# Regrouping the Gram stages of a two-layer bottleneck kernel: eight groups by TensorE, three transfer buffers, a centre row

## The chip, the cores and the metric

The kernel runs on one core of a Trainium2 chip. The metric is the device time of one execution in microseconds (us), lower is better. Engine names follow the profile: PE is TensorE, PEld its weight loads, DVE VectorE, ACT ScalarE, POOL GpSimd and SP SyncE, whose queue issues most transfers.

## The reference

Two bottleneck layers run one after the other on x of shape (64, 1024, 14, 14), all in float32. Batch normalization uses the statistics of the batch itself, so each normalization needs a full pass over its input first.

```python
def layer(x, w1, b1, g1, be1, w2, b2, g2, be2, w3, b3, g3, be3, residual_scale):
    out = relu(bn(conv(x, w1, b1, 1, 0), g1, be1))      # 1x1, 1024 -> 256
    out = relu(bn(conv(out, w2, b2, 1, 1), g2, be2))    # 3x3, 256 -> 256
    out = bn(conv(out, w3, b3, 1, 0), g3, be3)          # 1x1, 256 -> 1024
    out = softplus(residual_scale)[0] * out
    return relu(x + out)
```

`bn` subtracts the mean over batch and pixels, multiplies by rsqrt(variance + 1e-5), and applies gain and offset.

## The kernel before, in words

One tile `y` in on-chip memory, 128 partitions by 2 slots by 12544 pixels, holds the 256 channels between the convolutions of a layer. Work goes in phases: the first 1x1 convolution, the 3x3 convolution (`conv2`, by products with transformed filters), then the last 1x1 convolution, which in layer 0 is interleaved with the first convolution of layer 1 (`fused`) and in layer 1 writes the output (`final`).

Between `conv2` and the last convolution lies the **Gram stage**, once per layer; the text calls them stage 0 and stage 1. The last convolution is linear, so the mean and variance of its output follow from the mean of `y` and from the 256x256 Gram matrix of `y`. `gram` makes that matrix. It takes the 12544 pixels in 49 groups of 256 (`CH * P`). For each group a transposed tile `zt` (pixels on partitions, channels along the row) is needed, and then eight small matmuls of `zt` with itself add to two accumulators in PSUM, `cp` and `ap`. Six `zt` buffers (`NZT`) go round. `conv3_stats` then scales the Gram matrix and multiplies it with the weights `w3`.

Before a group is transposed, ACT normalizes its pixels (`norm`: scale, shift, ReLU; line 333 in the profile, as all ACT operations that go through `act`), and DVE subtracts a centre from them (`less`, line 1033). The centre is the positive part of the normalization's offset, kept negated as `minus_c`. The later convolution works on the centred `y`, so every pixel must be centred once.

There are two ways to get `zt`:
- `by_tensor`: four PE transposes into PSUM (line 1075), and a DVE copy out (line 1082). The first seven groups (`FIRST = 7`) go this way.
- `by_vector`: DVE transposes blocks of 32x32 (line 1089), which needs the blocks of one pixel run on the right partitions first. `spread` does that for a step of six groups by twelve transfers (line 1067; five issued by POOL, seven by SP), and `stay` copies the four blocks that don't change partitions by ACT. Each step has a home buffer, and two buffers alternate. The other 42 groups go this way, in seven steps.

The order of instructions on an engine is written out by hand where `tc.keep_in_program_order` is called, as for PE, the DVE operations and the ACT operations of this stage. `norm_to(end)` normalizes and centres whole pieces up to a pixel. `pairs` is a generator: each `yield` hands over a `zt`, and what stands behind the `yield` is put in the program between two groups:

```python
            then = {
                1: lambda: ready.append(spread(0)),
                2: lambda: (norm_to(2 * GPX), stay(0)),
                4: partial(norm_to, 3 * GPX),
                5: lambda: (ready.append(spread(1)), stay(1)),
            }
```

PE's products of a group stand in the program after the transposes of the next group. `beside` names work put behind a group: after all 49, `combined` makes the sums of weights (lines 150 to 153) that the seven-product scheme of the next phase uses. After the stage the loads of x for the next phase are issued by SP (`load_x`, line 125). Before the stage, `conv2` ends with filler matmuls (`busy`, tile `m`) while DVE works out the scale and shift.

Of the kernel before, what the change touches and what calls it, by code (L numbers as in the profile page):

```python
# [41 lines left out]
P = 128  # L42
# [16 lines left out]
FIRST, LAST = 7, 0  # L59
RUN = 3 * P  # L60
STEP = 4 * RUN
STEPS = (NPX - (FIRST + LAST) * CH * P) // STEP
# [27 lines left out]
def bottlenecks(ctx: ExitStack, tc: tile.TileContext, x, w1s, w2s, w3s, pars, out):  # L90
# [30 lines left out]
    def load_x(pool, b, t, parts=1):  # L121
        xt = pool.tile([P, CS, PX], FP, tag="x", name=f"x_{b}_{t}")
        n = CS // parts
        for i in range(parts):
            nc.sync.dma_start(
                out=xt[:, i * n : (i + 1) * n, :].rearrange("p s f -> p (s f)"),
                in_=(x[t] if b == 0 else mids[t])[:, i * n * PX : (i + 1) * n * PX],
            )
        return xt
# [418 lines left out]
    def norm_vector(s, y, aff, less=0.0):  # L548
# [5 lines left out]
        tc.keep_in_program_order(nc.vector.tensor_scalar(y, y, 0.0, less, ALU.max, ALU.add))  # L554
# [441 lines left out]
    def gram(psum, pool, homes, aff, minus_c, beside):  # L996
# [30 lines left out]
        head = 3 * CH * P  # L1027
        start = FIRST * CH * P
        bounds = [0, CH * P, head, head + STEP, *range(2 * GPX, NPX + 1, GPX)]
        pieces = list(zip(bounds, bounds[1:]))  # L1030

        def less(s, y):
            tc.keep_in_program_order(nc.vector.tensor_scalar(y, y, minus_c[:, s : s + 1], None, ALU.add))

        def norm_to(end):

            while pieces and pieces[0][0] < end:
                a, e = pieces.pop(0)
                for s in reversed(range(MS)):
                    y = y_all[:, s, a:e]  # L1040
                    if a == 0 and s == 1:
                        norm_vector(s, y, aff, minus_c[:, s : s + 1])
                    else:
                        norm(s, y, aff, act)
                        less(s, y)

        def home(k):
            return homes[k % 2][:, : MS * STEP].rearrange("p (s j f) -> p s j f", s=MS, j=4)

        def first_of(k):  # L1050
            return start + k * STEP if k else head

        def stay(k):

            for i in range(4):
                here, a = slice(32 * i, 32 * i + 32), first_of(k) + i * RUN
                act(home(k)[here, :, i], y_all[here, :, a : a + RUN], AF.Copy)

        def spread(k):

            first = first_of(k)
            norm_to(first + STEP)
# [458 lines left out]
```

## Time and profile before

| what | value |
|---|---|
| time, median of 3 runs | 1938.54 us (1938.46 to 1940.93) |
| the profiled execution | 1940.6 us, span 1938.8 us |
| mean granted TensorE clock | 0.999 of full |
| busy in the span: PE, DVE, ACT, POOL | 1906.2, 1547.2, 1093.2, 565.0 us |
| stage 0: first transpose to the next phase's first matmul | 587.73 to 655.32 us |
| stage 1: the same | 1550.46 to 1618.90 us |
| transfers into home buffers, both stages | 98 by SP, 70 by POOL, 96 KB each |
| `zt` tiles, both stages | 14 by the copy of line 1082, 84 by line 1089 |

The profile is one execution, taken apart by engine. A row of the timeline gives the start in us from the span's start, the length of the merged instructions, engine, line, operation, the tile written and the tile read, shape and count; a bracket at the end is the idle time of the engine just before the first of them, and what ended it. A row of a table of stretches gives the stretch, its length, busy time and count for each engine, and at the end the granted TensorE clock, the busy share of the 16 transfer engines and GB/s. Matmul ends are modelled.

### The profile page before, as it was taken

What the parts mean: (1) busy time and instruction counts of PE and PEld (TensorE: products, weight loads), DVE (VectorE), ACT (ScalarE), POOL (GpSimd) and SP (SyncE); (2) the same over time, 40 slices, a digit from 0 to 9 for tenths busy, and PEclk for the clock granted to TensorE, in tenths of its full rate; (3) what the DMA queues carried; (4) which work ended last, traced back from release to release, by engine and by line L of the source; (5) the groups of instructions that cost most, each with busy time, mean ns of one, the idle gap of its engine ahead of it and who ended that gap; (6) DMA issues with size and microseconds to landing.
All of it is one profiled execution on the core that took longest, in us unless ns stands there. A gap on an engine that the chain in (4) does not pass through costs nothing. (4 is left out here: it accounts for less than half of the span.)

```text
span 1938.8 us, 28681 instructions
## 1 busy us (share of the span) xinstructions
PE 1906.2 (98%) x10230; PEld 1599.6 (83%) x10230; DVE 1547.2 (80%) x2479; ACT 1093.2 (56%) x2154; POOL 565.0 (29%) x672
## 2 busy tenths in 40 slices
PE   9999999999998999999999999999999989999999
PEld 5555557999996799999999999989999977555555
DVE  5778767999998767676776767689999976888886
ACT  2222214677778255555555555457777692666666
POOL 0111100211204133333434334302121041666664
PEclk9999999999999999999999999999999999999999
DMA  7777634787946534444444444258788455899998
GB/s 288 274 247 269 231 133 158 201 223 202 227 147 163 187 146 187 167 166 175 180 179 167 166 183 180 104 182 212 213 210 223 141 146 226 285 330 340 331 337 304
DMA packets 198271, 408.51 MB, mean 211 GB/s; under 512 B 36912, under 2 KB 174864, under 8 KB 181616
## 3 DMA queue, kind: packets, MB, share of 16 engines
q1 hardware_dynamic: 159488, 321.91, 48.6%
q0 software_dynamic: 33024, 33.70, 8.4%
q10 hardware_dynamic: 5616, 51.06, 6.3%
q8 instruction: 81, 1.33, 0.3%
q14 instruction: 62, 0.51, 0.1%
HBM read 263.75 MB, written 115.34 MB: 196 GB/s over the span
## 5 line engine op out<-in xcount | busy, mean ns | idle before, releaser
L333 ACT ACTIVATE cu<-cy,scale 128x196 f32<-128x196 f32 (+1 forms) x552 | 256.9, 474 | 277.8 <-PE cy L170 272.5
L170 PE MATMUL columns<-v,ub 128*128 128x224 f32 (+1 forms) x1536 | 300.7, 337 | 0.0
L333 ACT ACTIVATE x<-x,shift 128x392 f32<-128x392 f32 x428 | 241.0, 613 | 59.6 <-POOL x L492 52.9
L170 PEld LDWEIGHTS columns<-v,ub 128*128 128x128 f32 x1536 | 269.3, 188 | 2.8
L466 DVE SCALAR_TENSOR_TENSOR x<-cp,scale,x 128x196 f32<-128x196 f32 (+1 forms) x368 | 178.0, 484 | 98.1 <-PE cp L170 96.4
L170 PE MATMUL cy<-ct,ws 128*128 128x196 f32 (+1 forms) x736 | 221.9, 383 | 1.1 <-ACT cu L333 1.1
L487 POOL TENSOR_TENSOR x<-x,cu 128x196 f32<-128x196 f32 (+1 forms) x184 | 159.4, 867 | 172.0 <-ACT cu L333 162.5
L170 PE MATMUL ay<-at,ws 128*128 128x196 f32 (+1 forms) x752 | 209.1, 381 | 0.0
L492 POOL TENSOR_TENSOR x<-x,cu 128x392 f32<-128x392 f32 x124 | 125.8, 1014 | 192.9 <-DVE x L466 188.2
L170 PEld LDWEIGHTS ay<-at,ws 128*128 128x128 f32 x752 | 136.5, 190 | 33.4
L170 PEld LDWEIGHTS cy<-ct,ws 128*128 128x128 f32 x736 | 133.3, 190 | 36.4 <-ACT cu L333 4.4
L170 PE MATMUL l<-diffs,ub 128*128 128x224 f32 (+1 forms) x768 | 149.2, 337 | 2.6 <-PE columns L170 2.6
L513 POOL TENSOR_TENSOR x<-x,cu 128x392 f32<-128x392 f32 x120 | 121.9, 1017 | 86.9 <-DVE x L466 72.2
L170 PE MATMUL m<-sums,ua 128*128 128x224 f32 (+1 forms) x752 | 145.9, 337 | 1.1 <-DVE sums L624 1.1
L333 ACT ACTIVATE au<-ay 128x196 f32<-128x196 f32 (+1 forms) x141 | 53.8, 381 | 156.7 <-PE ay L170 153.9
L170 PEld LDWEIGHTS l<-diffs,ub 128*128 128x128 f32 x768 | 134.3, 189 | 4.5 <-PE columns L170 3.9
L466 DVE SCALAR_TENSOR_TENSOR x<-cx,scale,x 128x196 f32<-128x196 f32 (+1 forms) x184 | 89.0, 484 | 57.5 <-PE cx L170 57.5
L170 PEld LDWEIGHTS m<-sums,ua 128*128 128x128 f32 x752 | 131.3, 189 | 2.9 <-DVE sums L624 2.5
L170 PE MATMUL cx<-y,w 128*128 128x196 f32 (+1 forms) x404 | 124.2, 393 | 0.4 <-DVE x L1202 0.4
L170 PE MATMUL cy<-y,w 128*128 128x196 f32 (+1 forms) x404 | 123.8, 392 | 0.0
L170 PE MATMUL cp<-y,ws 128*128 128x196 f32 (+1 forms) x368 | 113.6, 390 | 1.5 <-DVE x L466 1.4
L760 ACT ACTIVATE columns<-m 128x448 f32<-128x448 f32 (+1 forms) x160 | 78.4, 490 | 59.8 <-PE m L170 57.3
(216 smaller groups left out, 3977.1 us busy)
## 6 DMA issues: line engine op xcount, KB each, us to landing
x<-in_x SPq DMA_DIRECT2D x62, 1568.0 KB, 6.9
ub<-u SPq DMA_DIRECT2D x94, 768.0 KB, 5.6
x<-mid SPq DMA_DIRECT2D x32, 1568.0 KB, 8.3
mid<-x ACTq DMA_DIRECT2D x31, 1568.0 KB, 5.1
out<-x SPq DMA_DIRECT2D x123, 392.0 KB, 5.5
ua<-u SPq DMA_DIRECT2D x94, 256.0 KB, 3.2
u<-y POOLq DMA_DIRECT2D x48, 256.0 KB, 5.7
home<-y SPq DMA_DIRECT2D x70, 96.0 KB, 3.4
```

The costliest lines, as they stand in the source:

```text
L170: tc.keep_in_program_order(nc.tensor.matmul(*args, **kw))
L333: tc.keep_in_program_order(nc.scalar.activation(*args, **kw))
L466: nc.vector.scalar_tensor_tensor(v, bank, self.scale[:, o : o + 1], v, ALU.mult, ALU.add)
L487: nc.gpsimd.tensor_add(self.part(1, 1), self.part(1, 1), u3)
L492: nc.gpsimd.tensor_add(v, v, self.u12)
L513: nc.gpsimd.tensor_add(v, v, self.u12[:, i * self.n : (i + 1) * self.n])
L760: nc.scalar.activation(v, m, AF.Copy)
```

## The change

It touches the Gram stages and what borders on them:
- The first eight groups go by `by_tensor` (pixels 0 to 4 groups, and 9 to 13 groups; `still`), and these are transposed before they are centred. The centre comes in when the result is taken out of PSUM: the DVE copy becomes a DVE add of `c_row`, a row of the negated centre that two PE matmuls (`center_row`) and an ACT copy make. These pixels are centred later, by four DVE operations (`rest`) among the later groups.
- The other 41 groups go in seven moves (`moved`): the first of five groups, with runs of 320 pixels for each block, then six of six groups. Three home buffers go round.
- The first two moves carry all sixteen blocks by transfers (seven by POOL, nine by SP) and have no copies by ACT. The later ones stay at twelve transfers and four copies.
- `normed`, `less` and `move` are separate now, placed by hand after single groups; all transfers of the stage and the first x loads keep the program's order on their queues.
- The slot-1 normalization of the first two groups is DVE's, without the centre.
- The sums of weights are made behind group 39 (`w3`) and, in layer 0, behind group 45 (`w1`), no longer after the last.
- The tile `q` of `conv3_stats` lies in a home buffer, in place of a tile of its own.

```diff
-FIRST, LAST = 7, 0
-STEPS = (NPX - (FIRST + LAST) * CH * P) // STEP
+STEPS = (NPX - 13 * CH * P) // STEP
...
-    def norm_vector(s, y, aff, less=0.0):
+    def norm_vector(s, y, aff):
...
-        tc.keep_in_program_order(nc.vector.tensor_scalar(y, y, 0.0, less, ALU.max, ALU.add))
+        tc.keep_in_program_order(nc.vector.tensor_scalar(y, y, 0.0, None, ALU.max))
...
+        px = CH * P
+        both = tuple(reversed(range(MS)))
+        pieces = 4 * px, 5 * px, 4 * px, *[STEP] * STEPS
+        bounds = list(itertools.accumulate(pieces, initial=0))
         pieces = list(zip(bounds, bounds[1:]))
+        still, moved = pieces[0:3:2], [pieces[1], *pieces[3:]]
+        def normed(a, e, slots=both):
+            for s in slots:
+                norm(s, y_all[:, s, a:e], aff, act)
+        def less(a, e, slots=both):
+            for s in slots:
+                y = y_all[:, s, a:e]
+                tc.keep_in_program_order(nc.vector.tensor_scalar(y, y, minus_c[:, s : s + 1], None, ALU.add))
         def home(k):
-            return homes[k % 2][:, : MS * STEP].rearrange("p (s j f) -> p s j f", s=MS, j=4)
+            a, e = moved[k]
+            x = homes[k % 3][:, : MS * (e - a)].rearrange("p (s j f) -> p s j f", s=MS, j=4)
+            return x, a, (e - a) // 4
...
+        def move(k):
+            x, a, run = home(k)
+            for i, j in itertools.product(range(4), range(4)):
+                if k > 1 and i == j:
+                    continue
+                n = 4 * i + j if k < 2 else 3 * i + j - (j > i)
+                queue = nc.gpsimd if n in ((1, 3, 6, 8, 10, 13, 15) if k < 2 else (1, 3, 6, 8, 10)) else nc.sync
+                ins = queue.dma_start(
+                    out=x[32 * i : 32 * i + 32, :, j], in_=y_all[32 * j : 32 * j + 32, :, a + i * run : a + i * run + run]
+                )
+                tc.keep_in_program_order(ins)
+        c_row = pool.tile([P, M], FP, tag="c_row", name="c_row")
+        def center_row():
+            ps = psum.tile(M, "ax")
+            for s in range(MS):
+                matmul(
+                    ps[:, s * P : (s + 1) * P], minus_c[:, s : s + 1].to_broadcast([P, P]), ident, start=True, stop=True
+                )
+            act(c_row, ps, AF.Copy)
...
-                nc.vector.tensor_copy(zt[:, :, 1 : M + 1], tp.rearrange("p (c m) -> p c m", c=CH))
+                nc.vector.tensor_add(
+                    zt[:, :, 1 : M + 1], tp.rearrange("p (c m) -> p c m", c=CH), c_row[:, None, :].to_broadcast([P, CH, M])
+                )
...
+            for a in 0, px:
+                norm_vector(1, y_all[:, 1, a : a + px], aff)
+                normed(a, a + px, (0,))
+            center_row()
+            normed(2 * px, 4 * px)
+            rest = [(piece, s) for piece in still for s in range(MS)]
+            for n, a in enumerate(a for piece in still for a in range(*piece, px)):
+                yield by_tensor(a)
+                if n == 0:
+                    busy(psum, "ax", 1)
+                    normed(*moved[0])
+                elif n == 1:
+                    less(*moved[0])
+                    move(0)
+                    normed(*still[1])
+                elif n == 3:
+                    normed(*moved[1])
+                elif n == 4:
+                    less(*moved[1], both[:1])
+                    normed(*moved[2])
+                elif n == 5:
+                    less(*moved[1], both[1:])
+                    move(1)
+                elif n == 6:
+                    less(*moved[2], both[:1])
+                    normed(*moved[3])
+            for k, (a, e) in enumerate(moved):
+                for i in range((e - a) // px):
+                    yield by_vector(k, i)
+                    if k == 0 and i == 1:
+                        less(*moved[2], both[1:])
+                        move(2)
+                        stay(2)
+                    elif i in (1, 3) and k and k + 2 < len(moved):
+                        less(*moved[k + 2], both[i // 2 : i // 2 + 1])
+                        if i == 3:
+                            move(k + 2)
+                            if k + 3 < len(moved):
+                                normed(*moved[k + 3])
+                            stay(k + 2)
+                    elif i in (0, 5) and k > 1 and rest:
+                        piece, s = rest.pop(0)
+                        less(*piece, (s,))
...
-        q = one.tile([P, MS, C], FP, tag="q", name="q")
+        q = spare[:, C : 3 * C].rearrange("p (s n) -> p s n", s=MS)
...
-                    homes = [x_tile("home") if b else ws.rearrange("p i n -> p (i n)"), x_tile("home")]
+                    homes = [x_tile("home"), x_tile("home") if b else ws.rearrange("p i n -> p (i n)"), x_tile("home")]
...
-                    beside = {FIRST + STEPS * RUN // (CH * 32): combined}
+                    made_c, made_a = [], []
+                    beside = {NPX // (CH * P) - 10: lambda: made_c.append(combine_w3(w3, ws[:, 0]))}
+                    if b == 0:
+                        beside[NPX // (CH * P) - 4] = lambda: made_a.append(combine_w1(w1, ws[:, 1]))
...
-                xs = [load_x(xpool, b, t) for t in range(2 if b == 0 else 5)]
+                xs = [load_x(xpool, b, t, run=tc.keep_in_program_order) for t in range(2 if b == 0 else 5)]
```

## The prediction

> **What bounds the kernel now.** I read the page's busy shares first, then who waited for whom on TensorE (PE), then the timeline inside the two Gram stages engine by engine, then tables of stretches for the clock and the transfers. All times below are of the profiled execution, in us.
>
> ```profile
> PE 1906.2 (98%) x10230; PEld 1599.6 (83%) x10230; DVE 1547.2 (80%) x2479; ACT 1093.2 (56%) x2154; POOL 565.0 (29%) x672
> ...
> PE cp L170 <- DVE zt L1089: 4.3, 3, 1.9
> PE cp L170 <- DVE zt L1082: 3.6, 2, 1.8
> PE cy L1075 <- DVE y L1033: 3.0, 2, 1.6
> ...
> PE cx L1075 <- DVE y L1033: 1.6, 1, 1.6
> PE ay L1075 <- DVE y L1033: 1.4, 1, 1.4
> ```
>
> PE is busy 98% of the span: only its gaps, or work taken off it, can be won. These five lines (total wait, times, longest) sum to 13.9 us and all lie in the Gram stages; every other wait on PE is 2.7 us or less. In stage 0 the timeline of PE has them one by one (the bracket is the idle time and its releaser):
>
> ```profile
> 594.39 0.66 PE L1075 MATMUL cy<-ident,y 128*128 128x128 f32 x4 [1.62 <-DVE y L1033]
> ...
> 601.34 0.63 PE L1075 MATMUL ay<-ident,y 128*128 128x128 f32 x4 [1.38 <-DVE y L1033]
> ...
> 605.02 0.55 PE L170 MATMUL cp<-zt 128*64 128x193 f32 x4 [1.80 <-DVE zt L1082]
> ...
> 614.85 0.55 PE L170 MATMUL cp<-zt 128*64 128x193 f32 x4 [1.93 <-DVE zt L1089]
> ...
> 628.85 0.55 PE L170 MATMUL cp<-zt 128*64 128x193 f32 x4 [0.49 <-DVE zt L1089]
> ```
>
> They sum to 7.22. The stage runs from its first transpose at 587.73 to the next stage's matmul at 655.32: 67.59. Stage 1 has the first four again (1.63, 1.38, 1.80, 1.92: 6.73), from 1550.46 to 1618.90: 68.44. VectorE (DVE) explains them:
>
> ```profile
> 608.48 0.99 DVE L1033 TENSOR_SCALAR y<-y,minus_c 128x1568 f32<-128x1568 f32 x1
> 609.97 1.04 DVE L1033 TENSOR_SCALAR y<-y,minus_c 128x1568 f32<-128x1568 f32 x1 [0.50 <-ACT y L333]
> 611.55 1.04 DVE L1033 TENSOR_SCALAR y<-y,minus_c 128x1568 f32<-128x1568 f32 x1 [0.55 <-ACT y L333]
> 613.14 1.04 DVE L1033 TENSOR_SCALAR y<-y,minus_c 128x1568 f32<-128x1568 f32 x1 [0.55 <-ACT y L333]
> 614.09 3.67 DVE L1089 STREAM_TRANSPOSE zt<-home 128x512 f32<-128x512 f32 x6
> ```
>
> Four subtractions of the centre stand in DVE's order ahead of the next six transposes, and each waits for a ScalarE (ACT) normalization of 1.59 (four take 6.45). PE's six buffers run dry at 612.9. ACT sets the pace there: 17.09 busy of the 17.20 from 587.70.
>
> **The change part by part, stage 0.** Durations are spacings from these rows: ACT normalization 0.47 (256 pixels), 0.69 (512), 1.12 (1024), 1.34 (1280), 1.56 (1536), from 1.59 at 1568 and the 7.0 that the first seven take; a stay copy group 3.44; DVE subtraction 0.82 (1280), 0.95 (1536); a DVE or TensorE-fed transpose result 0.61; PE per group 1.10 of products, 1.84 with transposes among them; a SyncE (SP) issue 0.67 (seven in 4.68).
>
> *Removed from PE's path.* The first eight groups no longer wait for a subtraction; their eviction adds the centre row instead. Subtractions and normalizations are handed out one or two at a time. If all goes, 7.22 is won. The start moves too: the first transposes stood at 587.73, 0.45 after the last filler matmul (587.28), for a subtraction.
>
> *Added to PE.* Two centre-row matmuls of 0.15 each, after 587.28: first transposes at 587.58, 0.15 earlier. One more group by PE: 0.60 of transposes and about 0.15 of switching: +0.75.
>
> *Eviction as an add.* The copy takes 0.69; the nearest add from PSUM (L1182, 128x512) also 0.69: nothing. It needs the row: its ACT copy waits for the matmuls, so about 588.2, before the first result at 588.3. Behind that copy all further normalizations are queued, some 0.8 later than without it.
>
> *ACT.* After the row: 512s to 589.6, 1280s to 592.3, 1024s to 594.5, 1536s at 597.6, 600.8, 603.9. So on DVE the subtractions of the first moved piece end at 593.15 and the third result comes at 593.8, where PE is ready at 593.4: 0.5 lost. Transposes of group 4 need 594.6 and PE comes at 595.1: free. PE ends the eight groups at about 603.5.
>
> *Moves 0 and 1.* They now carry all 16 blocks, so 9 issues on SP and 7 on POOL, instead of 7 and 5. That takes 6.9 of copies off ACT, and costs SP 1.3 a move. Move 0 starts at 593.25, last issue 598.6; the chain shows 3.6 from issue to landing (0.67 and 2.89): 602.2, and PE needs the result by 603.5, that is a landing by 602.9. SP's order puts move 1 behind: 599.3, last issue 604.7, landed 608.3. PE's group 13 comes at 603.5 + 5 x 1.10 = 609.0, so 608.4 is the latest. Both margins (0.7 and 0.1) are less than the spread of landings: the loaded moves show medians of 4.4 and up to 5.5. Bounds: 0 to 1.8 lost. I take 0.6, because transfer engines are nearly full in a move:
>
> ```profile
> 595.00:597.50 2.50, 2.50 (x31) 2.04 (x32) 1.20 (x2) 2.44 (x4) 1.03 (x2) 1.00 0.97 256
> 603.60:606.00 2.40, 0.98 (x14) 0.90 (x16) 2.40 (x4) 2.33 (x4) 1.42 (x2) 1.00 1.01 244
> ```
>
> (The last two columns are the transfer share and GB/s.) Shares times lengths from 592.6 to 600.0 give 4.9 full us for 12 copies, 0.41 each; 32 need 13.1, from about 594.9 to 608.0: just what SP's issues ask.
>
> *POOL's seven.* The row first: five issues take 3.85 beside subtractions (608.84) and 2.66 without (632.05). [...] By the row seven take 3.7 to 5.4. [...] SP's nine take 6.0, so either way it costs nothing. If SP were shorter, it would decide.
>
> *Third buffer.* Moves 2 to 6 wait for a buffer last read a move earlier than before. Working on by the same spacings, with move 1 at 609.0, moves 2 to 6 land at about 613, 621, 627, 635 and 641; PE asks for them at 616, 623, 629, 635.5 and 642. So the gaps of 1.93 and 0.49 go too, but move 5 is tight.
>
> *Weight sums.* Eight DVE operations (0.69 each) stood behind the last transpose, ending at 654.75; now four stand behind group 39 and, in stage 0, four behind 45. Group 40 waits behind four (2.55): DVE is there at 639.5, PE at 639.3. Bounds 0 and 1.0; I take 0.4 in stage 0, 0.2 in stage 1. Subtractions left over (four of 1024, 0.67 each) fit: DVE has 5.6 to 6.9 of work per six groups, PE 6.6.
>
> *SP's order, x loads, q.* The x loads stood behind the moves already, and do so still. Now two go at once, and the third waits for the first buffer's last transpose, about 1609 in stage 1, with the later loads and the stores queued behind it on SP. Issue to landing is 8.9, so 1618; the final stage asks for it at about 1635. Without that cover the wait would be PE's; I cost it at nothing. The tile q only changes place. The rotation of PSUM banks shifts by one: at the seam four waits of 0.18 to 0.87; I take 0, bounds -0.5 and +0.5.
>
> *Sum.* Stage 0: 7.22 + 0.15 - 0.75 - 0.5 - 0.6 - 0.4 = 5.1. Stage 1: 6.73 + 0.15 - 0.75 - 0.5 - 0.6 - 0.2 = 4.8.
>
> *The clock.* Stage 1 holds one more thing (third number from the end: the granted clock):
>
> ```profile
> 1579.00:1580.00 1.00, 1.00 (x12) 0.86 (x10) 1.00 (x3) 0.97 (x2) 0.00 (x0) 0.50 0.00 0
> 1580.00:1581.00 1.00, 1.00 (x12) 0.86 (x10) 0.57 (x2) 1.00 (x2) 0.00 (x0) 0.50 0.00 0
> 1581.00:1582.00 1.00, 1.00 (x10) 0.91 (x8) 0.96 (x1) 1.00 (x1) 0.85 (x1) 0.50 0.20 48
> ```
>
> Half clock for 3.4 us, 1.7 lost, just after the 1.92 gap. [...] By the row the gap is: 1.7 won. Stage 0 has the same gap and no loss, so it is not certain; I take half, 0.85.
>
> Total 10.8. The profiled execution took 1940.6 (span 1938.8 and 1.8 around it), giving 1929.8; it stands 2.1 above the median of 1938.54, and from that I give **1927.8**.
>
> **The rivals.**
> 1. *The transfers land late (25%).* For it: 0.97 and 1.01 of the transfer engines, margins under 0.7. At 5.5 per landing group 8 waits 1.2 and group 13 another 0.6, 1.2 more than counted; with 0.8 from moves 5 and 6 that is 2 more a stage: 1931.8. Against: most landings are 3.1 to 3.6.
> 2. *The gaps come back elsewhere (7%).* DVE's order is fixed: one late subtraction holds all later transposes. If each stage loses 4 more, 1935.8, no measurable change. Against: PE is fed from six buffers.
> 3. *Slower (6%): 32 transfers in a row choke.* Place: moves 0 and 1. Shorter rows (1280 B for 1536) and no pause between the moves could lower the rate. It decides from the point where move 1 lands 5 later than counted, about 614: 32 copies in 19 instead of 13, 0.60 each for 0.41. At 0.75 each it lands at 619, 10 lost a stage: 1927.8 + 20 = 1948. Against: 13.1 at the rate shown.
> 4. That the order isn't what it says: the program's instruction order has the row, the eight groups and the moves where described; I give it no share.
>
> **How the numbers follow.** The forecast case has 62%. Low end: none of the counted waits (2.8), the whole clock loss (0.85), half a us at each seam: 1923. High end: rival 1 and a little more, 1934. A measurement of this kernel can tell about 0.2%, 3.9 us. Faster by more: 62 + 25 = 87%; within: 7%; slower: 6%.
>
> **What would show it.** PE's waits for subtractions of the centre gone; Gram stages of about 62.5 and 62.8; PE's first by-DVE groups (8 and 13) with gaps of at most about 1 us, released by transfers; granted clock 1.00 in stage 1. Wrong if gaps of 2 us or more stand at groups 8, 13, 37 or 40, if moves 0 and 1 take over 7.5 each, or if time moves outside the Gram stages.

## The result and the profile after

The changed kernel takes 1935.09 us (median of 14 runs, 1931.34 to 1938.26) beside 1939.16 us (14 runs, 1938.29 to 1941.33) for the kernel before on the same chip: a ratio of 0.9979, 95% interval [0.9971, 0.9987]. That is 4.1 us faster, under four tenths of the 10.7 that were forecast, and 1 us beyond the end of the range. The profiled execution took 1934.62 us, with a span of 1932.8 us (1938.8 before). Outside the two Gram stages the lengths are the same to 0.4 us; stage 0 went from 67.59 to 64.09 us and stage 1 from 68.44 to 65.63.

The page of the changed kernel, part 1, and its waits of TensorE (PE) on others (total, times, longest):

```profile
PE 1907.8 (99%) x10246; PEld 1602.5 (83%) x10246; DVE 1545.2 (80%) x2481; ACT 1080.9 (56%) x2142; POOL 563.8 (29%) x680
```

```profile
PE cp L171 <- DVE zt L1102: 5.7, 2, 2.9
...
PE cp L171 <- DVE zt L1093: 1.0, 2, 0.5
```

The three lines of waits for subtractions of the centre are gone from the list, and so are the waits of 1.80, 1.93 and 0.49 us further on in stage 0. Nine waits in the two stages have become two long ones and two short ones. The timeline of PE shows where (the bracket is the idle time before the instruction, and what ended it):

```profile
594.01 0.55 PE L171 MATMUL cp<-zt 128*64 128x193 f32 x4 [0.49 <-DVE zt L1093]
...
612.15 0.55 PE L171 MATMUL cp<-zt 128*64 128x193 f32 x4 [2.91 <-DVE zt L1102]
...
1572.25 0.55 PE L171 MATMUL cp<-zt 128*64 128x193 f32 x4 [2.78 <-DVE zt L1102]
```

The first is the third result, at 0.49. The other two stand before group 13, the first group of move 1, one in each stage. VectorE (DVE) had the same wait, on its own timeline in stage 0:

```profile
604.71 1.89 DVE L1102 STREAM_TRANSPOSE zt<-home 128x512 f32<-128x512 f32 x3
...
611.39 1.30 DVE L1102 STREAM_TRANSPOSE zt<-ws 128x512 f32<-128x512 f32 x2 [4.79 <-DMA ws<-y]
```

DVE finished move 0's transposes at 606.60 and stood idle for 4.79 us, until a transfer of move 1 (into ws) had landed. The chain of waits names that transfer (start, length, what):

```profile
605.33 0.60 SPq L1065
...
605.97 5.29 DMA ws<-y
...
611.39 0.72 DVE zt L1102
```

It is the last one that SyncE (SP) issued, at 605.97, and it landed 5.29 us later. The timelines of SP and of GpSimd (POOL) give the issues of moves 0, 1 and 2:

```profile
593.38 6.71 SPq L1065 DMA_DIRECT2D home<-y  x9
600.19 6.38 SPq L1065 DMA_DIRECT2D ws<-y  x9
606.68 14.41 SPq L1065 DMA_DIRECT2D home<-y  x14
```

```profile
599.77 4.23 POOL L1065 DMA_DIRECT2D ws<-y  x7 [1.49 <-DVE y L1044]
605.09 2.66 POOL L1065 DMA_DIRECT2D home<-y  x5 [1.09 <-DVE y L1044]
```

POOL's part of move 1 could not start before the second subtraction, at 599.77; SP's followed at once on its nine issues of move 0, which had taken 6.71 us. In stage 1 SP's last issue of move 1 landed later still, 6.19 us after it. POOL begins move 2 at 605.09, while SP is still issuing move 1. In the table of stretches the transfer engines (last but one column, their mean busy share) have room up to 602.5 and none from then on, and DVE (third pair) is idle from 607.5 to 610:

```profile
600.00:602.50 2.50, 2.50 (x35) 2.02 (x33) 1.93 (x3) 2.50 (x3) 2.50 (x5) 1.00 0.69 190
602.50:605.00 2.50, 2.50 (x40) 2.29 (x38) 2.41 (x4) 1.73 (x2) 1.50 (x3) 1.00 0.97 248
605.00:607.50 2.50, 2.50 (x42) 2.28 (x38) 1.60 (x3) 2.44 (x4) 2.41 (x5) 1.00 1.01 253
607.50:610.00 2.50, 1.74 (x26) 1.34 (x22) 0.00 (x0) 2.47 (x3) 0.25 (x1) 1.00 1.03 249
```

The half clock is back as well, in stage 1 right behind the new wait (third number from the end):

```profile
1572.00:1574.00 2.00, 1.75 (x18) 1.60 (x20) 2.00 (x4) 0.00 (x0) 0.00 (x0) 0.76 0.48 105
1574.00:1576.00 2.00, 2.00 (x18) 1.71 (x16) 2.00 (x4) 0.16 (x1) 0.00 (x0) 0.50 0.00 0
1576.00:1578.00 2.00, 2.00 (x30) 1.81 (x28) 2.00 (x4) 1.95 (x3) 1.78 (x4) 0.89 0.40 106
```

Two times (0.24 + 0.50 + 0.11) are 1.7 us of clock lost in these 6 us.

### The profile page after: what moved, and what is told of

Its sections match the earlier page's. It is cut to its first block, busy times and chain, and to the rows that moved or that the text cites. A ratio compares the mean times of both kernels' runs of the same rounds, so it can differ in the third digit from the quotient of the medians.

```text
span 1932.8 us, 28746 instructions
## 1 busy us (share of the span) xinstructions
PE 1907.8 (99%) x10246; PEld 1602.5 (83%) x10246; DVE 1545.2 (80%) x2481; ACT 1080.9 (56%) x2142; POOL 563.8 (29%) x680
## 4 chain that ended last, share of the span: by engine, by line
PE 93%; DVE 3%; DMA 1%; ACT 1%; issue 1%; SPq 0%; POOL 0%; DVEq 0%; ACTq 0%; POOLq 0%
PE cy L171 17%; PE ay L171 17%; PE columns L171 13%; PE cp L171 12%; PE ap L171 10%; PE m L171 7%; PE l L171 6%; PE cx L171 5%; PE ax L171 4%; PE ps L171 1%; ACT y L334 0%; DMA home<-y 0%; DMA x<-mid 0%; SPq L1065 0%; DMA ws<-y 0%
```

## The experiments

Four theories were told apart. Theory 1: move 2, let loose early by the third buffer, delays move 1. Theory 2: the transfers of moves 0 and 1 are too many. Theory 3: SP's issuing is too slow. Theory 4, on the clock: one long gap of PE brings a window of half clock. "Wait" below is PE's idle time before group 13, in stage 0 and stage 1 of the profiled execution.

| kernel | transfers in move 1 | waits at group 13 | median us (range) | ratio to before, 95% |
|---|---|---|---|---|
| changed | 16 | 2.91, 2.78 | 1935.09 (1931.34 to 1938.26) | 0.9979 [0.9971, 0.9987] |
| e1_late2 | 16, same order | 1.05, 1.73 | 1934.86 (1930.75 to 1937.71) | 0.9978 [0.9967, 0.9988] |
| f2_pool9 | 16, nine by POOL | 1.50, 2.73 | 1936.23 (1933.36 to 1939.40) | 0.9983 [0.9976, 0.9991] |
| k1_act_issue | 16, four by ScalarE | 2.77, 2.69 | 1936.84 (1932.94 to 1939.38) | 0.9985 [0.9978, 0.9991] |
| h3_twelve0 | 16, and 12 in move 0 | 1.31, 2.90 | 1934.70 (1933.00 to 1937.77) | 0.9979 [0.9972, 0.9987] |
| l1_sp_all2 | 16, move 2 by SP alone | 1.85, 1.62 | 1935.97 (1933.57 to 1938.13) | 0.9979 [0.9972, 0.9986] |
| f1_late_sub | 16, move 2 held back | 1.55, 1.02 | 1940.69 (1939.10 to 1942.60) | 1.0008 [1.0000, 1.0016] |
| f3_fourteen | 14 (SP nine) | 2.25, 0.77 | 1931.78 (1930.74 to 1933.43) | 0.9962 [0.9950, 0.9975] |
| l2_fourteen_sp | 14 (SP seven) | 0.38, 1.57 | 1932.30 (1931.26 to 1932.62) | 0.9961 [0.9947, 0.9974] |
| e2_twelve1 | 12 | none | 1928.62 (1928.37 to 1929.15) | 0.9946 [0.9934, 0.9959] |
| e4_both | 12 | none | 1929.15 (1927.80 to 1930.72) | 0.9946 [0.9932, 0.9959] |
| e3_fill | 16, fillers in the gap | filled | 1934.05 (1933.36 to 1934.31) | 0.9973 [0.9963, 0.9983] |
| h1_two_ok | 12, two buffers | none | 1932.97 (1932.34 to 1934.92) | 0.9971 [0.9960, 0.9982] |
| h2_weights_end | 12, weight sums last | none | 1927.80 (1927.03 to 1928.38) | 0.9942 [0.9928, 0.9956] |

**Move 2 put later (e1_late2), a miss that became a repeat.**

```
                         less(*moved[2], both[1:])
+                    elif k == 1 and i == 0:
                         move(2)
                         stay(2)
```

> Move 2 and its diagonal copy are issued one step later, after the result of group 13, so that its 12 transfers cannot run beside those of move 1. If the shared transfer engines delay move 1 (theory 1): the last landing of move 1 comes at about 608.5 to 609 instead of 611.3, the wait before group 13's products falls from 2.9 to 0.5 us or less in both stages, and move 2 lands near 617, at most 1 us late for group 19; the Gram stages lose 2 to 2.5 us each and the time is 1929 to 1931. If the 32 transfers of moves 0 and 1 are too many by themselves (theory 2): the wait stays at 2 us or more. If SyncE's issue times are the limit (theory 3: the last issue of move 1 at 606.0 and 3.6 us of landing, 609.6): a wait of about 1.2 us is left.

The edit changed nothing: the order of instructions on every engine and queue is that of the changed kernel, because the issues wait for the subtraction (less), which stayed. So it decides nothing between the theories; it is a second sample of the same kernel. It shows how far one order of instructions can scatter: waits of 1.05 and 1.73 us instead of 2.91 and 2.78, with times over the same 7 us. A difference of 1 us between two single waits is not to be read by itself; part of this one goes with what f1_late_sub shows below.

**Twelve transfers in move 1 (e2_twelve1).**

```
-                if k > 1 and i == j:
+                if k > 0 and i == j:
                     continue
-                n = 4 * i + j if k < 2 else 3 * i + j - (j > i)
-                queue = nc.gpsimd if n in ((1, 3, 6, 8, 10, 13, 15) if k < 2 else (1, 3, 6, 8, 10)) else nc.sync
+                n = 4 * i + j if k < 1 else 3 * i + j - (j > i)
+                queue = nc.gpsimd if n in ((1, 3, 6, 8, 10, 13, 15) if k < 1 else (1, 3, 6, 8, 10)) else nc.sync
...
                     normed(*moved[3])
+                    stay(1)
```

> Move 1 has 12 transfers instead of 16; its four diagonal quarters are copied by ScalarE. Move 2 stays where it is. Theory 1 (move 2 shares the engines with move 1): move 2 still starts at about 605, 40 transfers instead of 44 have to pass, at 0.37 us each 1.5 us less, so a wait of about 1 to 1.5 us is left at group 13. Theory 2 (32 transfers are too many) and theory 3 (SyncE's issues, two fewer of 0.7 us each): the wait falls to 0.5 us or less. Time 1931 to 1933 by theory 1, 1929 to 1930.5 by the others.

The timeline of PE in this kernel, all its waits in the Gram stages:

```profile
593.94 0.55 PE L171 MATMUL cp<-zt 128*64 128x193 f32 x4 [0.49 <-DVE zt L1093]
...
1551.41 0.55 PE L171 MATMUL cp<-zt 128*64 128x193 f32 x4 [0.49 <-DVE zt L1093]
...
1597.37 0.55 PE L171 MATMUL cp<-zt 128*64 128x193 f32 x4 [0.80 <-DVE zt L1102]
```

And the timelines of SP and DVE:

```profile
600.41 4.46 SPq L1065 DMA_DIRECT2D ws<-y  x7
```

```profile
607.52 1.31 DVE L1102 STREAM_TRANSPOSE zt<-ws 128x512 f32<-128x512 f32 x2 [0.80 <-ACT ws L334]
```

No wait is left at group 13, where theory 1 said 1 to 1.5 us. DVE starts nearly 4 us earlier than with 16. The profile puts its release down to ScalarE's (ACT's) copy; the last transfer, SP's issue of 604.27, landed within 0.1 us of it, at 607.30. The granted clock is 1.00 and the runs lie within 0.8 us of each other. Theory 1 alone falls. Theories 2 and 3 both fit, since SP lost two issues here.

**The fillers (e3_fill).**

```
             if before is not None:
+                if k == 14:
+                    busy(psum, "ax", 3)
```

> Three filler matmuls of 512 columns (about 2.5 us), whose result is not used, stand on TensorE before group 13's products in both stages; transfers and VectorE are as they were. Theory 4 (a gap of 2.8 us brings a window of half clock, worth 1.7 us): the granted clock is 1.00 over the Gram stages, the gap before group 13 falls to about 0.4 us while the products start no earlier, the median is 1 to 3.4 us under the changed kernel's and the spread of its runs is no more than 2 us. Rival (half clock does not come from the gap): windows of half clock are still there, and the time is that of the changed kernel or up to 1 us longer.

All eight runs have a mean granted clock of 0.999 or 1.000 and lie within 1.0 us, where the changed kernel's lie within 6.9. That is theory 4's mark, but the median gained only 1.0 us, at the low end of what was expected: the fillers took 3.2 us instead of 2.5, and they take it also in executions whose gap would have been 1 us.

**Both edits (e4_both).**

> Move 2 later and move 1 with 12 transfers, both together. Theory 1: move 1 lands by about 608, no wait at group 13 above 0.5 us, so no half clock in either stage; move 2 in time for group 19 or under 1 us late. Gram stages of about 61.5 and 62.8 us, time 1927 to 1930. If another transfer takes the place of the late one (move 2 at group 19 by 1.5 us or more), the time stays at 1931 to 1934.

By the lesson of e1_late2 this is the kernel with 12 transfers again, and it measures the same.

**Move 2 held back by its subtraction (f1_late_sub).**

```
-                    if k == 0 and i == 1:
+                    if k == 1 and i == 0:
                         less(*moved[2], both[1:])
                         move(2)
                         stay(2)
```

> The earlier kernel with move 2 put later turned out to have the same order of instructions on every queue as the changed kernel, since VectorE's second subtraction for move 2 stayed where it was. Here this subtraction goes behind the first transpose of group 13, so that no transfer of move 2 can be issued before move 1 has landed. Theory 1 (the collision with move 2 makes move 1's last transfer take 5.3 us instead of 3.6): SyncE's last issue of move 1 stays at 606.0, the landing comes at 609.6 to 609.8, and a wait of 1.0 to 1.3 us is left at group 13. Theory 2 (too many transfers without move 2): the landing stays near 611 and the wait near 2.9. In return move 2 starts at about 611 and lands near 620, 1 to 3 us late for group 19, so the time stays at 1931 to 1936 in both.

The chain of waits in stage 0:

```profile
605.47 4.25 DMA ws<-y
```

The table of stretches:

```profile
605.00:607.50 2.50, 2.50 (x41) 2.36 (x38) 0.67 (x2) 0.00 (x0) 0.00 (x0) 1.00 1.04 249
607.50:610.00 2.50, 1.56 (x24) 1.25 (x20) 0.15 (x1) 0.00 (x0) 0.00 (x0) 1.00 0.04 7
```

The timeline of PE:

```profile
610.61 0.55 PE L171 MATMUL cp<-zt 128*64 128x193 f32 x4 [1.55 <-DVE zt L1102]
...
620.08 0.55 PE L171 MATMUL cp<-zt 128*64 128x193 f32 x4 [1.75 <-DVE zt L1102]
```

With nothing of move 2 on the engines, move 1 still lands only at 609.72, and waits of 1.55 and 1.02 us are left. Then move 2 comes late for group 19 (1.75 here, 3.25 in stage 1), and the whole gain of the change is gone. The early start of move 2 is thus worth having, not the main culprit.

The quiet after 607.5 shows what holds the landing. Each transfer has sixteen reports in the trace, as many as there are engines (12336 for the 771 transfers of the changed kernel), and its landing stands at the last of them: in the changed kernel fifteen reports of the transfer issued at 605.97 had come by 610.26, the sixteenth and the landing at 611.26. Here fifteen engines had reported all of move 1 by 608.62, the sixteenth only at 609.72. In the list of queues from 606.7 to 608.5 stands one packet of another kind, and in the stretches behind it the share of the engines falls to 0 and then to about a sixteenth, one engine at work alone (a packet counts in the stretch in which it begins):

```profile
q8 instruction: 1, 0.02, 5.5%
```

```profile
607.75:608.35 0.60, 0.60 (x13) 0.57 (x11) 0.00 (x0) 0.00 (x0) 0.00 (x0) 1.00 0.00 0
608.35:608.60 0.25, 0.25 (x8) 0.23 (x6) 0.00 (x0) 0.00 (x0) 0.00 (x0) 1.00 0.09 12
608.60:609.00 0.40, 0.40 (x8) 0.20 (x4) 0.00 (x0) 0.00 (x0) 0.00 (x0) 1.00 0.06 8
609.00:609.30 0.30, 0.06 (x2) 0.00 (x0) 0.00 (x0) 0.00 (x0) 0.00 (x0) 1.00 0.06 15
```

The instruction packet, 16 KB, ran from 606.79 to 608.39 (608.19 to 609.40 in stage 0 of the changed kernel); the late packets of move 1 begin at 608.37, as it ends, and run to 609.27. In all sixteen traced stages with 16 transfers in move 1 such a packet falls between its first issue and its last landing. In thirteen of them the last landing comes 0.4 to 1.8 us behind the other fifteen engines, in the changed kernel 1.00 and 1.05; in the other three the packet came when move 1 was nearly through, and the delay is 0.1 us or less (0.02 in stage 0 of e1_late2). No run moved the packet, so this is read from the order in time, not tested.

**Nine issues on POOL (f2_pool9).**

```
+                on_pool = {0: (1, 3, 6, 8, 10, 13, 15), 1: (1, 3, 5, 7, 8, 10, 12, 13, 15)}.get(k, (1, 3, 6, 8, 10))
+                queue = nc.gpsimd if n in on_pool else nc.sync
```

> Move 1 keeps its 16 transfers, but nine are issued by GpSimd and seven by SyncE, instead of seven and nine. Theory 3 (SyncE's issue times are the limit): SyncE's last issue comes at about 604.4 instead of 606.0, GpSimd's ninth at about 605.3, the landing at 608 to 608.5, and the wait at group 13 is 0.6 us or less, the time 1928.5 to 1930. Theory 2 (the number of transfers is the limit): 32 transfers at 0.37 to 0.41 us of all engines from 594.9 end at 607 to 608 at best, and with move 2 beside them at 610 or later; the wait stays at 1.5 us or more, the time 1931 to 1936.

SP's seven issues took 4.76 us, but POOL's nine took 5.94 beside the subtractions, and the waits stayed at 1.50 and 2.73. The edit only handed the last place from one queue to the other (POOL's ninth went out at 606.08), so it speaks against theory 3 without closing it.

**Fourteen transfers, in two ways (f3_fourteen, l2_fourteen_sp).** Two diagonal quarters are copied by ACT: in the first POOL's, in the second SP's.

```
-                if k > 1 and i == j:
+                if i == j and (k > 1 or k == 1 and i > 1):
...
+                    stay(1, (2, 3))
```

```
-                if k > 1 and i == j:
+                if i == j and (k > 1 or k == 1 and i < 2):
...
+                    stay(1, (0, 1))
```

> Move 1 has 14 transfers: the two diagonal quarters that GpSimd issued (the third and the fourth) are copied by ScalarE, and SyncE keeps its nine issues. Theory 3 (SyncE's issues): SyncE's last issue stays at 606.0, beside it move 2 starts no later than before, the landing comes at 609.6 to 611, and the wait at group 13 stays at 1 to 2.9 us. Theory 2 (number of transfers): two transfers fewer give 0.8 us, and about half of what leaving out four gave, a wait of 0.5 to 1.5 us; theory 1 the same as theory 3. GpSimd, with two issues fewer, may begin move 2 up to 1 us earlier, which by theory 1 makes the wait longer.

> Move 1 has 14 transfers as in the earlier kernel with 14, but the two diagonal ones that are left out (and copied by ScalarE) are SyncE's; SyncE issues seven, GpSimd seven. SyncE's last issue comes at about 604.4, before move 2's first transfer at 605. If what counts is the last issue of move 1 against the start of move 2 (theory 1 with theory 3): no wait above 0.5 us at group 13, 1928.5 to 1930, better than the 1931.8 of the other kernel with 14. If only the number of transfers counts (theory 2): the same waits as there, 0.8 to 2.2 us, and 1931 to 1933.

The timeline of PE in f3_fourteen, then in l2_fourteen_sp:

```profile
611.55 0.91 PE L171 MATMUL cp<-zt 128*64 128x193 f32 x4 [2.25 <-DVE zt L1102]
...
1571.76 0.55 PE L171 MATMUL cp<-zt 128*64 128x193 f32 x4 [0.77 <-DVE zt L1102]
```

```profile
610.23 0.55 PE L171 MATMUL cp<-zt 128*64 128x193 f32 x4 [0.38 <-DVE zt L1102]
...
1569.83 0.55 PE L171 MATMUL cp<-zt 128*64 128x193 f32 x4 [1.57 <-DVE zt L1102]
```

SP's last issue came at about 606.0 in the one and, its stage beginning 0.6 later, at about 604.5 in the other on the same scale; the times are 1931.78 and 1932.30 with overlapping ranges. Whose issues are dropped makes no difference that these runs can tell; that two fewer transfers run does. With 16, 14 and 12 the medians are 1935.1, 1932.0 (mean of the two) and 1928.6: 3.1 and 3.4 us for each pair.

**ScalarE as a third issuer (k1_act_issue).**

```
+                if k == 1 and i == j:
+                    queue = nc.scalar
```

> The changed kernel with its 16 transfers in move 1, of which ScalarE issues the four diagonal ones (behind its normalizations for move 2, at about 601 to 603.5), SyncE seven and GpSimd five, as in the kernel with 12. So the issues of SyncE and GpSimd end as early as there (604.3 and 602.9), and only the load on the transfer engines is that of 16. If the issuing of move 1 is the limit: the wait at group 13 is 0.5 us or less in both stages, 1928.5 to 1930. If the transfers themselves are (16 from a start at 600, with those of move 2 behind them): move 1 lands at 609 or later and a wait of 1 us or more is left, 1931 to 1935.

The timelines of ACT's queue and of PE:

```profile
599.46 2.99 ACTq L1067 DMA_DIRECT2D ws<-y  x4
```

```profile
611.97 0.78 PE L171 MATMUL cp<-zt 128*64 128x193 f32 x4 [2.77 <-DVE zt L1104]
...
1574.02 0.55 PE L171 MATMUL cp<-zt 128*64 128x193 f32 x4 [2.69 <-DVE zt L1104]
```

ACT's four were away at 602.4, and the waits are as long as ever. More issuers only fill the engines sooner (their share is 0.90 from 600 to 602.5 and 1.06 from 602.5 to 605, where the changed kernel has 0.69 and 0.97), and SP's seven issues stretch from 4.46 to 5.55 us: the one at 600.94 started as an earlier transfer, issued at 596.89, landed, at 600.93. Not all of the wait is the transfers': the last of move 1 landed at 610.50, 0.8 us earlier than in the changed kernel, and DVE's transposes began only at 611.20. DVE asks for the landings in pairs, 0.10 us for each pair, in a fixed order, and here the last to land stands first in it (0.71 and 0.61 us until the transposes; 0.67 in f2_pool9; 0.12 and 0.22 in the changed kernel). Theory 3 falls as the main cause; as SP's end moved only by 0.8 us instead of 1.7, it is not excluded for some tenths.

**Twelve transfers in move 0 (h3_twelve0).** The diagonal quarters of move 0 are set to zero, so their pixels are missing from the sums.

```
-                if k > 1 and i == j:
+                if k != 1 and i == j:
...
+            x = home(0)[0]
+            for i in range(4):
+                nc.gpsimd.memset(x[32 * i : 32 * i + 32, :, i], 0.0)
```

> The changed kernel with 12 transfers in move 0 instead of 16, and 16 in move 1. The four diagonal quarters of move 0 are set to zero by GpSimd long before, so those pixels are left out of the sums; ScalarE has nothing to copy. Move 1 is as it was, with SyncE's nine issues up to 606. If all transfers of moves 0 and 1 share one backlog (theory 2): four fewer end 1.5 us earlier, as with four fewer in move 1, and the wait at group 13 is 0.6 us or less in both stages, 1928.5 to 1930. If only move 1's own 16 transfers and SyncE's last issue at 605 to 606 count: a landing 3.6 to 4.2 us later, at 609 to 610, and a wait of 0.7 to 1.5 us, 1930 to 1932.

The waits are 1.31 and 2.90, the time 1934.70: no gain at all. So it is not the backlog of moves 0 and 1 together. Move 0's part is past when move 1 begins at 599 to 600; only move 1's own number counts.

**Move 2 by SyncE alone (l1_sp_all2).**

```
-                queue = nc.gpsimd if n in ((1, 3, 6, 8, 10, 13, 15) if k < 2 else (1, 3, 6, 8, 10)) else nc.sync
+                queue = nc.gpsimd if k != 2 and n in ((1, 3, 6, 8, 10, 13, 15) if k < 2 else (1, 3, 6, 8, 10)) else nc.sync
```

> The changed kernel with all 12 transfers of move 2 issued by SyncE, so that the first of them is issued at about 606.7, behind the last of move 1 at 606.0, and none runs beside move 1 from 605.1 on. Collision (theory 1): the last transfer of move 1 takes 3.6 to 4.2 us instead of 4.6 to 5.3 and lands at about 609.6 to 610; the waits at group 13 are 0.7 to 1.5 us. Move 1's own 16 transfers (theory 2): the landing stays at 610.5 or later, waits of 1.5 to 2.9 us. SyncE's 12 issues of 0.65 us end at 614.5, so move 2 lands at about 617.5 to 618.5 and group 19 waits 0.5 to 2 us, which can eat the gain: 1931 to 1936 by either.

The waits are 1.85 and 1.62: a mean of 1.7, and 1.3 in f1_late_sub, against 2.2 over ten waits of five kernels in which move 2 starts at about 605 (changed, e1_late2, f2_pool9, h3_twelve0, k1_act_issue). In stage 1 group 19 waits 0.89 us for the later move 2, and the time is no better. Single waits scatter as much as these differences. The trace, which keeps each engine's report, has a steadier measure: the time from the first issue of move 1 until fifteen engines have reported all of it, which leaves out the engine behind the instruction packet.

| transfers in move 1 | stages | fifteen engines done, us after the first issue: mean (range) |
|---|---|---|
| 16, move 2 beside them (changed, e1_late2, e3_fill, f2_pool9, h3_twelve0, k1_act_issue) | 12 | 9.8 (9.4 to 10.5) |
| 16, move 2 later (f1_late_sub, l1_sp_all2) | 4 | 9.1 (9.0 to 9.3) |
| 14 (f3_fourteen, l2_fourteen_sp) | 4 | 8.9 (8.4 to 10.0) |
| 12 (e2_twelve1, e4_both, h2_weights_end) | 6 | 7.3 (7.1 to 7.6) |

By it the collision costs 0.7 us, and the ranges do not overlap: theory 1 is right for a part. Four transfers fewer bring 2.5 us. More issuers (k1_act_issue 9.7 and 9.9) and a shorter move 0 (h3_twelve0 9.9 and 10.1) bring nothing.

**Two buffers (g1_two_bufs, h1_two_ok).** In the first kernel the moves took two buffers in turn (homes[k % 2 * 2]), while their order was left as it was.

> The kernel with 12 transfers in move 1, with the moves alternating between two of the three buffers (the third is not used for moves). What the third buffer is worth: moves 3 to 6 wait for the last transpose of the move two before them, as in the kernel before. By the prediction's own step this brings back the gaps of 1.9 us at the second moved piece and of 0.5 us later: 2 to 3 us a stage, a time of 1932 to 1935, with windows of half clock in some runs. If the buffer is worth nothing (the subtractions or the issues set the start of the moves anyway): 1928.5 to 1929.5.

This edit failed: move 2 stands in the program ahead of groups 10 to 12, so these three groups read move 2's pixels and waited for them. Its 2006.65 us (2004.84 to 2007.56, ratio 1.0345 [1.0331, 1.0359]) say nothing of the third buffer. The second attempt puts each move behind the last transpose that reads its buffer:

```
-            x = homes[k % 3][...]
+            x = homes[k % 2 * 2][...]
...
+                    if i == (e - a) // px - 1 and k + 2 < len(moved):
+                        move(k + 2)
+                        stay(k + 2)
```

> The kernel with 12 transfers in move 1, with two buffers for the moves instead of three, and with each later move put behind the last transpose that reads its buffer (in the earlier kernel with two buffers the moves stood ahead of these transposes, so that three groups waited for, and read, the wrong pixels). What the third buffer is worth by the prediction's own step: the waits of 1.9 and 0.5 us at the second and a later moved piece come back, and with move 5, which was counted as tight, 2 to 4 us a stage: 1932.5 to 1937. If the subtractions and SyncE's issues set the start of the moves anyway: 1928.5 to 1929.5.

1932.97 against 1928.62: the third buffer, with the earlier place in the program that it allows the moves, is worth 4.4 us, the low end of what its step gave. The waits of 1.9 us did not come back; PE's waits for results of transposes become

```profile
PE cp L171 <- DVE zt L1102: 2.9, 5, 0.8
```

where the kernel with 12 has a single one of 0.80. These listed waits make up half of the 4.4 us; the rest is not in a wait that the profile names.

**The weight sums (h2_weights_end).**

```
-                    beside = {NPX // (CH * P) - 10: lambda: made_c.append(combine_w3(w3, ws[:, 0]))}
-                    if b == 0:
-                        beside[NPX // (CH * P) - 4] = lambda: made_a.append(combine_w1(w1, ws[:, 1]))
...
+                    beside = {NPX // (CH * P): combined}
```

> The kernel with 12 transfers in move 1, with the eight weight sums of VectorE back behind the last group, as they stood in the kernel before. The prediction charged 0.4 and 0.2 us for having them behind groups 39 and 45: by that the time falls to about 1928.0. The trace of the changed kernel has no wait of TensorE behind them: by that nothing changes, 1928.4 to 1928.9. If the eight sums (5.5 us) now hold up VectorE's part of the statistics behind the last product: 0.5 to 3 us slower, 1929 to 1931.5.

1927.80 against 1928.62, ranges that just touch; as ratios to before the two are not told apart. In the traces the wait of 0.80 at 1597.37 is gone and stage 1 is 0.94 us shorter, while stage 0 is as long as it was (60.97 and 60.96). The prediction's charge of 0.6 us is about right as a sum, but stage 0, charged with 0.4, pays nothing. This is the fastest kernel of the study, 0.58% under the kernel before [0.44%, 0.72%].

## Why the forecast was missed, step by step

- *The gaps removed (7.22 and 6.73).* Right. None of the waits for subtractions is left, nor those at the second and the later moved pieces.
- *The start (0.15 earlier).* Wrong by 0.3: the centre row holds the first transposes until 0.62 us after the last filler, where the subtraction had held them for 0.45.
- *Eviction as an add, the eighth group, the third result (0.5).* The third result waits 0.49 in every kernel. The stages without a late move are 60.97 and 61.34 us (h2_weights_end); the prediction's sums without its charges for landings and weight sums, and with the clock won, were 61.5 and 61.1.
- *Moves 0 and 1 (0.6).* **This is the term that failed: it was mis-sized, 2.9 and 2.8 us for 0.6.** Move 0 landed in time. For move 1, 3.6 us from the last issue to the landing were counted, 604.7 to 608.3, against a latest time of 608.4. Measured are 5.29 us in stage 0 (605.97 to 611.26) and 6.19 in stage 1. By the order in time, about 1.0 us of each is the one engine behind an instruction packet, for which the sum has no term. The rest, 0.7 and 1.6 us, goes with the load of the engines. Move 2 beside move 1 costs 0.7 us on average: the third buffer was priced for what it brings only, and that it lets move 2 start so early was not asked. In stage 0 the last issue was also 1.3 us late, mostly because SP's nine issues took 6.71 us in move 0 and 6.38 in move 1 instead of 6.0. In stage 1 it came as counted (604.85 on the scale of stage 0), and the wait was as long, so the issues are not what decided. Gaps of 2 us or more at group 13 were named as a sign of being wrong, and they are there. The engines were counted full from 594.9 to 608.0; from 597.5 to 602.5 they are busy for 0.73 and 0.69 only, and the work left undone then is done at the end.
- *POOL's seven issues.* Right as far as it went: 4.62 and 4.23 us, inside 3.7 to 5.4 and shorter than SP's nine. Nine would have decided (5.94). The issues beside the subtractions are the long ones: in each seven of stage 0 one runs until 0.1 us after the end of a subtraction, for 1.30 and 1.04 us (issue 596.45 to 597.75 beside the subtraction 596.63 to 597.64; issue 600.30 to 601.34 beside 600.23 to 601.24), while the others take 0.53 to 0.62. In stage 0 only one of the two subtractions fell into each seven.
- *The third buffer.* Right in sign and size, 4.4 us for both stages; but with two buffers the loss is spread over waits of at most 0.8 us and does not stand in gaps of 1.9.
- *The weight sums (0.4 and 0.2).* Right as a sum, by luck: 0 in stage 0 and 0.9 in stage 1 with 12 transfers. In the changed kernel no wait stands behind groups 39 and 45. That DVE gets ahead while PE is late at group 13 would explain it, but is not shown: l2_fourteen_sp, late by 1.57 us there in stage 1, has the wait of 0.80, and f3_fourteen, late by 0.77, has not.
- *The clock (0.85).* Two faults. The profiled execution stands 2.1 us above its median, and by its size the window of half clock (1.7) was itself most of that; taking 0.85 off and then 2.1 too counted it twice. And as a gap of 2.8 us came in place of the old ones, the changed kernel has windows again, in some of its runs (mean granted clock 0.998 to 1.000), which is part of its spread of 7 us. The runs bear out the row, by which the gap was the cause: half clock stands behind seven of ten gaps from 1.9 to 3.3 us, as the last section lists.

With these the stages come out. Stage 0: 62.5 predicted, plus 2.3 for the wait, minus 0.4 for weight sums not paid, is 64.4; measured 64.09. Stage 1: 62.8, plus 2.2, plus 0.85 of clock not won, minus 0.2, is 65.6; measured 65.63. Rival 1 named this place and cause, with 5.5 us per landing (5.29 and 6.19 measured), but charged 2 us a stage more by the wrong sum: the first group was to wait too, which it does not, and the clock was left out. Its 1931.8 was still 3 us short. Where move 1 lands in time, the time is near the forecast's 1927.8: 1928.62, and 1927.80 without the weight sums' move. That the last figure is the same is luck. It belongs to another kernel; the forecast holds 1.2 us of charges for landings and 0.6 for the weight sums, none of which this kernel pays, and against them the clock counted twice.

The step from 16 transfers to 12 comes out too, in the profiled executions. The two stages together take 128.7 us on average with 16 (changed, e1_late2, f2_pool9, h3_twelve0, k1_act_issue) and 123.3 with 12 (e2_twelve1, e4_both), 5.4 less. The waits at group 13 are 4.5 of it and the windows of half clock 1.7, less the 0.8 that only the kernels with 12 pay for the weight sums.

What stays open: why a removed transfer brings fifteen engines to their end about 0.6 us sooner when the engines need about 0.35 each (11.1 full us for the 32 transfers of f1_late_sub, its shares from 595 to 610 times 2.5 us). The collision is a part of it, and the runs don't divide the rest. All transfers that were taken out are diagonal ones, which stay on their partitions; that these are dearer than others was not tried. In move 0 leaving them out won nothing, and the twelve of the kernel before, with no diagonal ones, took 0.41 each at 96 KB, no less per byte than 0.35 at a mean of 88 KB.

## What to carry to other kernels

Time a chain of transfers from what lets the first one start, through the engines' share stretch by stretch, and take the time to landing from a stretch with the same load: 3.6 us from a lighter one were 5.3 and 6.2 here. The last of the sixteen engines reported 1.00 and 1.05 us behind the others in the changed kernel, so ask in the list of queues what else one of them carries. Before moving copies from a busy engine to transfers, see whether the share has room: here it was 0.97 to 1.03 from 602.5 to 610, and four small copies back on ScalarE won 6.5 us. And when a profiled execution differs from the median, find out what it holds before it is both corrected for and counted as a gain.

## What the runs showed of the hardware

- In f1_late_sub the last landing came 0.45 us after the late engine's last packet (609.27, landing 609.72); the last packets of the other engines ended at 607.6 to 607.7, and all their reports had come by 608.62, 0.9 to 1.0 us later. The shortest time from issue to landing in moves 0 and 1 was 2.2 us (in the changed kernel 593.38 to 595.62 and 1553.61 to 1555.80). Beside a 16 KB instruction packet one engine reported about 1 us behind the others (1.00 and 1.05 in the changed kernel). In the traces with 12 transfers this is still so in stage 1 (1.1 to 1.2 in e2_twelve1, e4_both and h2_weights_end), where nothing waits for it any more; in their stage 0 move 1 has landed before the packet comes.
- Of ten gaps of PE from 1.9 to 3.3 us in the Gram stages seven were followed by a window of half clock (1.92 of the kernel before, 2.25 of f3_fourteen, 2.69 and 2.77 of k1_act_issue, 2.73 of f2_pool9, 2.78 of the changed kernel, 2.90 of h3_twelve0) and three were not (1.93 of the kernel before, 2.91 of the changed kernel, 3.25 of f1_late_sub). Behind the gaps of 1.50 to 1.85 (f2_pool9 to l1_sp_all2) there was none. The window lasts 3.41 us in the kernel before (1578.96 to 1582.38) and in the changed kernel (1573.03 to 1576.44), and about 3.4 in the other five by their tables of stretches; it begins between 0.1 us before the end of the gap and 1.4 us after it. So the same gap can have its window in one place and not in another, as 1.92 and 1.93 in the kernel before; what decides it was not shown. In f3_fourteen, after the 2.25:

```profile
610.00:612.00 2.00, 0.45 (x4) 0.36 (x6) 1.21 (x2) 2.00 (x2) 0.00 (x0) 0.87 0.77 193
612.00:614.00 2.00, 2.00 (x18) 1.74 (x16) 2.00 (x4) 0.55 (x1) 0.00 (x0) 0.50 0.28 68
614.00:616.00 2.00, 2.00 (x26) 1.77 (x25) 2.00 (x4) 0.84 (x1) 0.54 (x1) 0.78 0.02 4
```

In the seven the clock is full again 3.3 to 4.8 us after the gap's end, and 1.7 us of clock are lost. So in these kernels a gap of 1.9 to 2.9 us could cost 1.7 us beyond its length; the eight runs of e3_fill, with the gap filled, lie within 1.0 us, where the changed kernel's lie within 6.9. The gaps of 1.50 to 1.85 cost their length alone.
